# Two ways to transpose the inputs of tiles 8 to 15: on TensorE through PSUM, or on VectorE in 32x32 blocks put in place over DRAM

## The chip, the cores and the metric

The kernel runs on one core of a Trainium2 chip. The metric is the device time of one execution in microseconds; the median of a few executions is what counts. The engines are named as the profile names them: PE (TensorE) with its weight loads PEld, DVE (VectorE), ACT (ScalarE), POOL (GpSimd) and SP (SyncE, which here does nothing but issue DMAs; the profile writes SPq for its queue). Each engine takes its own instructions in order. Here that order is written out by hand for every engine.

## What is computed

Two layers with a residual sum each. The first mixes the 32 rows of a batch by a 32x32 matrix that its condition picks; the second is paged attention with new keys and values beside the cached ones.

```python
W = weights[condition]
x = x + einsum('bct,bcd->bdt', x, W)                # x: 64 batches x 32 rows x 512

q, k, v = x @ Wq.T, x @ Wk.T, x @ Wv.T              # 32 query heads, 8 key heads of 128
q, k = rope(rmsnorm(q)), rope(rmsnorm(k))
kc, vc = k_cache[block_table], v_cache[block_table] # 512 cached rows of a batch
probs = softmax(where(valid, q @ [kc, k].T * SCALE, -1e30))
x = x + (probs @ [vc, v]) @ Wo.T
```

All of it is float32.

## The kernel before

**Tiles, steps, slots.** The 2048 rows of x make 16 tiles of 128 rows (four batches of 32 rows: BT = 4, S = 32). The 8 key heads are taken in two halves of four. So there are 32 steps: steps 0 to 15 are tiles 0 to 15 with the first half of the heads, steps 16 to 31 the same tiles with the second half. The loop at L1549 gives each step 16 slots, one for each of its four batches and four units of scores. In a slot PE does one unit of scores against cached keys (`scores`, L1020), then what is planned for this slot (the dictionaries `plan`, `ahead` and `after_plan`, filled by `at`, L1342, and `later_of`), then the product with cached values of the slot before (`values`, L1081). Planned work is the preparation of later tiles and the output projection of earlier ones.

**The input of a tile.** Before the projections, a tile's rows have to be mixed with the condition matrix, added to themselves and transposed, so that the 512 inputs lie on the partitions: `x1t`, 128 partitions x 4 chunks x 128 rows. This is made once, in the first half, and kept in DRAM (`x1t_d`) for the second half. `input_of` (L1357) plans it: load the condition's blocks (`load_cond_weights`), load the rows (`x1_a`), mix (`x1_c`: one matmul of 128x512 on PE, an addition on DVE), transpose (`x1_b`, L411: four 128x128 transposes on PE into PSUM, one copy by ACT into SBUF). After `KEEP` = 2 slots the mixed rows go to `acc_d` (`keep_x1`, L428) and `x1t` goes to `x1t_d` (`keep_x1t`, L425), both issued by SP.

**Pairs.** From tile 4 on, tiles are projected in pairs by a seven-product scheme (`products`, L686). The two `x1t` of a pair are the four quarters A11, A12 (first tile) and A21, A22 (second tile) of one SBUF tile, `early`; there is only one such tile. `sums_x` (L665) makes S1 = A21 + A22 and S2 = S1 - A11 (L668, L669, slot 2 of step n), then S4 = A12 - S2 and S3 = A11 - A21 (L671, L672, slot 3). S3 is written over A21, so L672 has to wait until `keep_x1t` of the second tile has read it. The next DVE instruction in this slot is T2 (`t2`, L725), the difference of two weights. PE's product 6, S2 times T2 (`pb`, L697), stands in slot 5.

**Where the inputs stand.** A pair of tiles s0 and s0 + 1 is projected from step n = s0 - 2 on, and its inputs are made in step n - 1. For tiles 8 to 15 that is steps 5, 7, 9 and 11. There the mixing stood in slots 11 and 12 and the transposes in slots 13 and 14, while slots 9 to 13 also hold the last products of the output projection of two earlier tiles (`p67`, `p4_of`, L836), which wait for weight differences by DVE (L906, L907, L911).

**Cached keys.** SP loads a batch's cached keys in two halves of eight DMAs of 64 KB each (`load_k`, L312, DMAs at L321) into three buffers, the first half in the first and the second in the third slot of a batch, two batches ahead. Before each first half it loads the page numbers into its registers (L301). DVE copies the keys head by head (L1017, `kh`), four slots before PE needs them. The columns of queries come back from DRAM over SP as well (`spread`, L546, DMAs at L552).

**A block transpose that is there already.** The projected queries and keys are transposed without PE: `turn_rows` (L535) turns 32x32 blocks by DVE (L540, 128x512), POOL stores the result to `heads_d` with one DMA (L544), and `spread` loads it with the blocks in place. The buffer is `slab`, or in some slots `pn`, which is also where `new_scores` (L1040) puts its weights in slot 0 of each step.

POOL also gathers the cached values (L354, two in every second slot) and does part of the norm (L487, L488).

Of the kernel before, what the change touches and what calls it, by code (L numbers as in the profile page):

```python
# [12 lines left out]
F32 = mybir.dt.float32  # L13
# [7 lines left out]
P = 128  # L21
B, S, HID = 64, 32, 512
# [6 lines left out]
BT = P // S  # L29
NT = B // BT  # L30
# [3 lines left out]
KC = HID // P  # L34
# [26 lines left out]
def cond_resid_paged_attention_kernel(  # L61
# [23 lines left out]
    nc = tc.nc  # L85
# [3 lines left out]
    dram = ctx.enter_context(tc.tile_pool(name="dram", bufs=1, space=DRAM))  # L89
# [27 lines left out]
    part = const.tile([P, 1], F32, tag="part", name="part")  # L117
# [62 lines left out]
    def other_half(by):  # L180
# [2 lines left out]

    x1t_d = [
        dram.tile([P, KC * P], F32, tag=f"x1t_d{t}", name=f"x1t_d{t}") for t in range(NT)
    ]
    acc_d = [dram.tile([P, HID], F32, tag=f"acc_d{t}", name=f"acc_d{t}") for t in range(NT)]
    rot_d = {
# [14 lines left out]
    def steps_of(exact, pools):  # L203
        def pool(name, bufs, **kw):
            return pools.enter_context(
                tc.tile_pool(name=f"{name}_{int(exact)}", bufs=bufs, **kw)
            )
# [4 lines left out]
        work = pool("work", 2)  # L212
# [71 lines left out]
        def load_cond_weights(t, eng=nc.sync, kind=mybir.EngineType.SP):  # L284
            number = conditions(t, kind)
            for i in range(BT):
                blk = slice(i * S, (i + 1) * S)
                eng.dma_start(
                    bds[t % 2][blk, blk],
                    w_cond.rearrange("(n s) e -> n s e", s=S)[bass.ds(number[i], 1)].rearrange(  # L290
                        "o s e -> (o s) e"
                    ),
                )
# [89 lines left out]
        def x1_a(st):  # L383

            if st.pair is None:
                tag = "sums" if st.n and not exact else "acc"
                st.acc = work.tile([P, HID], F32, tag=tag, name=f"acc_{st.name}", bufs=2)
            else:
                i = st.n % 2
                if i == 0:  # L390
                    st.pair.read = work.tile(
                        [P, 2, HID], F32, tag="os", name=f"read_{st.name}", bufs=1
                    )
                st.acc = st.pair.read[:, i]
            src = acc_d[st.t] if st.hh else x[st.t * P : (st.t + 1) * P, :]
            nc.sync.dma_start(st.acc, src)
# [7 lines left out]
        def x1_c(st):  # L404
            if st.hh:
                return
            pm = ps_p.tile([P, 512], F32, tag="pp", name=f"pmix_{st.name}")
            nc.tensor.matmul(pm, bds[st.t % 2], st.acc, start=True, stop=True)
            nc.vector.tensor_tensor(st.acc, pm, st.acc, ALU.add)

        def x1_b(st):  # L411
            if st.hh:
                return
            pm = ps_p.tile([P, KC, P], F32, tag="pp", name=f"px1t_{st.name}")
            for c in range(KC):
                nc.tensor.transpose(pm[:, c, :], st.acc[:, c * P : (c + 1) * P], ident)
            if st.pair is None:
                st.x1t = work.tile(
                    [P, KC, P], F32, tag="x1t" if exact else "u3", name=f"x1t_{st.name}", bufs=1
                )  # L420
            nc.scalar.copy(st.x1t, pm)
            if st.n or exact:
                kept.append(lambda: keep_x1t(st, nc.sync))

        def keep_x1t(st, eng):  # L425
            eng.dma_start(x1t_d[st.t], st.x1t.rearrange("p c q -> p (c q)"))

        def keep_x1(st, eng=nc.sync):  # L428
            eng.dma_start(acc_d[st.t], st.acc)
# [103 lines left out]
        kept, in_slots = [], []  # L533
# [123 lines left out]
        def pair_x(pair):  # L657
            pair.x = early.rearrange("p (i c q) -> p i c q", i=7, c=2)
            for i, st in enumerate(pair.both):
                st.x1t = pair.x[:, 2 * i : 2 * i + 2].rearrange("p a c q -> p (a c) q")  # L660

        def load_x(st):
            nc.sync.dma_start(st.x1t.rearrange("p c q -> p (c q)"), x1t_d[st.t])
# [18 lines left out]
        def shift_w(hh, k):  # L682
            b11, _, b12, _ = halves(hh, k)
            nc.vector.tensor_tensor(b12, b12, b11, ALU.subtract)
# [135 lines left out]
        class Both:  # L820
# [123 lines left out]
            t = None  # L944
# [393 lines left out]
        for pair in pairs:  # L1338
            pair_x(pair)
        plan, ahead, after_plan = (defaultdict(list) for _ in range(3))  # L1340

        def at(n, slot, *work_of):  # L1342
            plan[n, slot].extend(work_of)
# [13 lines left out]
        def input_of(st, n, load, weights, mix, turned_at):  # L1357
            at(weights[0], weights[1], lambda: load_cond_weights(st.t))
            if load:
                at(load[0], load[1], lambda: x1_a(st))  # L1360
            at(n, mix, lambda: x1_c(st))
            at(n, turned_at, lambda: x1_b(st), lambda: kept.append(lambda: keep_x1(st)))

        def set_of(pair, k, n, slots):
            pieces = products(pair, k)
            for slot, names in slots.items():
                for name in names.split():
                    at(n, slot, pieces[name])
# [45 lines left out]
        for pair in pairs:  # L1414
            s0, s1 = pair.both
            n = s0.n - 2
            if n == 2:
                input_of(s0, 2, (1, 15), (1, 15), 4, 5)
                input_of(s1, 2, None, (2, 2), 6, 7)
                ahead[2, 1].append(lambda st=s1: x1_a(st))  # L1420
                at(2, 8, lambda: shift_w(0, 0))
                at(2, 9, lambda pair=pair: sums_x(pair))
                angles_of(2, 1, 9, 9)
                tables_of(pair, "q", 2, 8)
                tables_of(pair, "k", 3, 2)
                set_of(pair, 0, 2, {9: "t2", 10: "1", 11: "6 2 t3", 12: "5 t4", 13: "3 7", 14: "4"})
                at(3, 1, lambda: shift_w(0, 1))
                set_of(pair, 1, 3, {2: "t2", 3: "1 6 t3", 4: "2 5 t4", 5: "3", 6: "7", 7: "4"})
                at(3, 6, lambda: shift_w(0, 2))
                set_of(  # L1430
                    pair, 2, 3,
                    {8: "t2 1", 9: "2 t3", 10: "6 t4", 11: "7", 12: "4", 13: "5", 14: "3"},
                )
                spread_of(s0, 3, (12, 12, 13, 13))
            else:
                at(n, 2, lambda pair=pair: sums_x(pair, (0,)))
                at(n, 3, lambda pair=pair: sums_x(pair, (1,)))
                if pair.hh:
                    at(n - 1, 7, lambda st=s0: load_x(st))
                    at(n - 1, 10, lambda st=s1: load_x(st))  # L1440
                    tables_of(pair, "q", n - 1, 6)
                    tables_of(pair, "k", n, 7)
                else:
                    late = int(n == 4)
                    m = (n - 1, 7)
                    input_of(s0, n - 1, m, (n - 1, 6), 11 + 3 * late, 13 + 2 * late)
                    input_of(s1, n - 1, m, (n - 1, 7), 12 + 2 * late, 14 + late)
                    angles_of(s0.n // 2, n - 1, 4, 4 if late else 6)
                    if late:
                        tables_of(pair, "q", n, 1)  # L1450
                        tables_of(pair, "k", n, 4)
                    else:
                        tables_of(pair, "q", n - 1, 6)
                        tables_of(pair, "k", n, 11)
                if s0.n == NT:
                    at(n, 1, lambda: shift_w(1, 0))
                    at(n, 8, lambda: shift_w(1, 1))
                    at(n + 1, 3, lambda: shift_w(1, 2))
                set_of(
                    pair, 0, n,  # L1460
                    {3: "t2 1", 4: "2", 5: "6", 6: "5 t3", 7: "3 t4", 8: "7", 9: "4"},
                )
                set_of(
                    pair, 1, n,
                    {10: "t2", 11: "1", 12: "6 2 t3", 13: "5 t4", 14: "7 3", 15: "4"},
                )
                set_of(
                    pair, 2, n + 1,
                    {4: "t2 1", 5: "2 t3", 6: "6 t4", 7: "7", 8: "4", 11: "5", 13: "3"},
                )  # L1470
                spread_of(s0, n + 1, (10, 10, 11))
                ahead[n + 1, BT - 1].append(lambda st=s0: spread(st, BT - 1))
            spread_of(s1, n + 2, (3, 5, 8))
            ahead[n + 2, BT - 1].append(lambda st=s1: spread(st, BT - 1))
# [16 lines left out]
        valued, turned = (batch, GH - 1), [batch]  # L1491
# [57 lines left out]
        for st in steps:  # L1549
            for bt in range(0 if st.n else 1, BT):  # L1550
# [3 lines left out]
                for g in range(GH):  # L1554
# [39 lines left out]
                    if slot == (14 if st.n - 1 in twos else 10):  # L1594
# [4 lines left out]
                        turned = []  # L1599
# [16 lines left out]
                    if slot == 0 or slot == 13 and st.n - 1 not in twos or slot == 15:  # L1616
                        for ba in turned:
                            turn(ba)
                        turned = []
# [81 lines left out]
```

## Time and profile before

| | us |
|---|---|
| median of three executions | 2082.15 |
| the three | 2078.98, 2082.15, 2083.43 |
| the profiled execution | 2077.26 |
| span of the profiled execution, first to last instruction | 2075.5 |
| mean granted TensorE clock in it | 0.997 |
| one step (start of the new scores to the next), steps 5 to 12 | 62.4 to 65.1 |

The profiled execution ran 2077.26 us, 1.8 us more than its span, and 4.9 us less than the median of the three executions.

Busy time by step, for the four steps in which the inputs of tiles 8 to 15 are made and the four after them, from the view of windows:

| step | window, us | PE | PEld | DVE | ACT | POOL | share of DMA engines |
|---|---|---|---|---|---|---|---|
| 5 | 396 to 461 | 64.62 | 53.49 | 57.75 | 31.22 | 33.45 | 0.66 |
| 6 | 461 to 523 | 62.00 | 46.98 | 50.26 | 30.84 | 33.93 | 0.74 |
| 7 | 523 to 588 | 64.95 | 53.90 | 58.19 | 32.11 | 33.29 | 0.66 |
| 8 | 588 to 650 | 62.00 | 46.98 | 50.52 | 29.96 | 33.37 | 0.72 |
| 9 | 650 to 714 | 64.00 | 53.07 | 57.10 | 31.83 | 32.32 | 0.63 |
| 10 | 714 to 776 | 62.00 | 47.10 | 50.30 | 30.22 | 34.53 | 0.75 |
| 11 | 776 to 840 | 63.98 | 52.92 | 57.10 | 31.55 | 33.01 | 0.64 |
| 12 | 840 to 902 | 62.00 | 47.10 | 50.39 | 30.43 | 33.33 | 0.81 |

How to read the profile: a row of the timeline has its start and its length in microseconds, the engine and the line, what is written from what, the shape, how many instructions were merged, and in brackets the idle time before it with what ended it. A float32 matmul of the program runs as two matmul records, a transpose as one. Matmuls overlap in the pipeline, so that the length of one (273 ns for a transpose) is more than what it adds to PE's time; the chain of waits shows the latter.

### The profile page before, as it was taken

The page shows a single profiled execution, that of the slowest core. Times are in us where ns is not written, and L with a number is a line of the kernel's source. Part 1 is how long each engine was busy: PE and PEld are TensorE (multiplying, and loading weights), DVE is VectorE, ACT ScalarE, POOL GpSimd, SP SyncE. Part 2 cuts the span into 40 slices and gives each one's busy share as a digit, 9 for nine tenths or more (in the row PEclk, how much of TensorE's full clock was granted, in tenths as well). Part 3 has the DMA queues.
Part 4 walks back from the last instruction along what each step waited for, and adds up shares of the span by engine and source line. Part 5 has one row for each costly group of instructions (what it writes and reads, how often), then busy time and mean ns, then how long its engine had stood idle before and what let it go on. Part 6 is the DMA issues. An engine that isn't in the chain of part 4 may idle for free.

```text
span 2075.5 us, 45239 instructions
## 1 busy us (share of the span) xinstructions
PE 2042.3 (98%) x13428; PEld 1587.7 (76%) x13428; DVE 1630.7 (79%) x3532; ACT 958.4 (46%) x2707; POOL 991.2 (48%) x1122
## 2 busy tenths in 40 slices
PE   7999999999999999999999999999999999999998
PEld 4767667787887878878786677878878787787886
DVE  4555687988979789797997769889797987979744
ACT  4444354544545444544534445344454434545441
POOL 4354465545636465463544436355353544535331
PEclk9999999999999999999999999999999999999999
DMA  8767557667676676787767876676767667676672
GB/s 245 202 177 219 160 153 230 183 190 220 186 218 188 195 215 189 220 264 217 222 193 201 241 212 184 201 207 179 209 184 211 188 195 211 178 215 182 191 212 78
DMA packets 410255, 413.33 MB, mean 199 GB/s; under 512 B 58928, under 2 KB 325552, under 8 KB 410000
## 3 DMA queue, kind: packets, MB, share of 16 engines
q1 hardware_dynamic: 354096, 229.87, 39.1%
q0 software_dynamic: 55168, 180.27, 28.9%
q8 instruction: 109, 1.79, 0.4%
q14 instruction: 146, 1.20, 0.2%
q10 hardware_dynamic: 736, 0.21, 0.0%
HBM read 350.09 MB, written 60.03 MB: 198 GB/s over the span
## 4 chain that ended last, share of the span: by engine, by line
PE 80%; DVE 6%; DMA 6%; SPq 4%; issue 2%; POOL 1%; ACT 1%; DVEq 0%; ACTq 0%; POOLq 0%
PE ps_x L1026 18%; PE po_x L1089 18%; PE p_x L836 14%; PE pb_x L697 8%; PE pc_x L697 6%; PE pa_x L697 6%; PE pout_x L793 4%; SPq L321 3%; DMA k_t_x<-in_kt_dram 2%; PE pnv_x L1071 2%; PE pp_q_x L470 2%; PE psn_x L1047 1%; DMA q_ring_x<-heads_d 1%; PE pp_v_x L470 1%; DMA wq_x<-in_wq_dram 1%
## 5 line engine op out<-in xcount | busy, mean ns | idle before, releaser
L354 POOL DMA_INDIRECT raw_x<-in_vc_dram,v_row x512 | 548.3, 1071 | 639.8 <-ACT v_ring_x L366 518.4
L1037 ACT ACTIVATE pr_x<-ps_x 128x512 f32<-128x512 f32 x511 | 305.7, 598 | 779.1 <-PE ps_x L1026 774.1
L1089 PEld LDWEIGHTS po_x<-v_ring_x,pr_x 128*128 128x128 f32 x4088 | 522.9, 191 | 86.8 <-issue 66.2
L1026 PE MATMUL ps_x<-q_ring_x,kh_x 128*128 128x128 f32 x4088 | 546.4, 276 | 1.6 <-ACT q_ring_x L611 1.6
L1089 PE MATMUL po_x<-v_ring_x,pr_x 128*128 128x129 f32 x4088 | 543.5, 275 | 3.2 <-DVE nv_x L1100 2.8
L1026 PEld LDWEIGHTS ps_x<-q_ring_x,kh_x 128*128 128x128 f32 x4088 | 498.7, 192 | 13.8 <-issue 3.1
L366 ACT ACTIVATE v_ring_x<-raw_x,valid 128x512 f32<-128x512 f32 x512 | 342.7, 714 | 19.8 <-DMA raw_x<-in_vc_dram,v_row 19.2
L1017 DVE COPY kh_x<-k_t_x 128x512 f32<-128x512 f32 x506 | 219.8, 435 | 97.6 <-PE ps_x L1026 67.2
L544 POOL DMA_DIRECT2D heads_d<-rows_x x150 | 126.2, 842 | 280.8 <-DVE rows_x L540 215.9
L697 PE MATMUL pb_x<-t_x,early 128*128 128x512 f32 x504 | 238.2, 595 | 2.0 <-DVE u_x L713 1.1
L1100 DVE TENSOR_TENSOR nv_x<-po_x,nv_x 128x258 f32<-128x258 f32 x256 | 106.9, 417 | 100.7 <-PE po_x L1089 96.1
L836 PEld LDWEIGHTS p_x<-wo_x,ot_x 128*128 128x128 f32 x624 | 116.5, 190 | 62.3 <-issue 45.9
L488 POOL TENSOR_TENSOR rs_q_x<-ms_q_x,minus_half 128x4 f32<-128x4 f32 x128 | 158.8, 1241 | 10.7
L836 PE MATMUL p_x<-wo_x,ot_x 128*128 128x256 f32 x624 | 156.3, 380 | 0.1
L836 PE MATMUL p_x<-ts_x,ot_x 128*128 128x256 f32 x624 | 145.6, 380 | 0.7 <-DVE ts_x L911 0.7
L697 PEld LDWEIGHTS pb_x<-t_x,early 128*128 128x128 f32 x504 | 86.2, 191 | 64.8 <-issue 61.9
L836 PEld LDWEIGHTS p_x<-ts_x,ot_x 128*128 128x128 f32 x624 | 115.4, 190 | 25.3 <-issue 8.4
L1103 DVE TENSOR_TENSOR nv_x<-nv_x,rden 128x256 f32<-128x256 f32 x256 | 109.6, 428 | 8.7
L479 ACT ACTIVATE sq_q_x<-u_x 128x128 f32<-128x128 f32 x224 | 66.2, 298 | 94.0 <-DVE u_x L713 94.0
L697 PE MATMUL pc_x<-wq_x,early 128*128 128x512 f32 x224 | 105.4, 593 | 0.0
L697 PE MATMUL pa_x<-wq_x,early 128*128 128x512 f32 x224 | 105.4, 593 | 0.0
L514 DVE TENSOR_TENSOR rope_q_x<-rope_q_x,rs_q_x 128x512 f32<-128x512 f32 x120 | 82.3, 686 | 19.8 <-POOL rs_q_x L488 19.3
(203 smaller groups left out, 2612.0 us busy)
## 6 DMA issues: line engine op xcount, KB each, us to landing
k_t_x<-in_kt_dram SPq DMA_DIRECT2D x2048, 64.0 KB
heads_d<-rows_x POOLq DMA_DIRECT2D x150, 256.0 KB
q_ring_x<-heads_d SPq DMA_DIRECT2D x480, 80.0 KB
raw_x<-in_vc_dram,v_row POOLq DMA_INDIRECT x512
wo_x<-in_wo_dram SPq DMA_DIRECT2D x32, 256.0 KB
res_x<-acc_d SPq DMA_DIRECT2D x31, 256.0 KB
wq_x<-in_wq_dram SPq DMA_DIRECT2D x8, 512.0 KB
early<-x1t_d SPq DMA_DIRECT2D x16, 256.0 KB
```

What stands on the lines that cost most here:

```text
L354: nc.gpsimd.indirect_dma_start(out=raw.rearrange("p g d -> p (g d)"), out_offset=None, in_=vc, in_offset=bass.IndirectOffsetOnAxis(ap=v_ro ...
L366: nc.scalar.activation(v_ring[:, c, :, 0:D], raw, AF.Copy, scale=valid[:, b, c : c + 1])
L488: nc.gpsimd.tensor_tensor(rs, ms, minus_half, ALU.pow)
L544: nc.gpsimd.dma_start(heads_d[st.n][:, :, i, :].rearrange("k p c -> p k c"), part)
L697: nc.tensor.matmul(bank, pair.x[:, i, c, :], by[:, c * 512 : (c + 1) * 512], start=start and c == 0, stop=c == 1, skip_group_check=not start,)
L836: nc.tensor.matmul(to, left[:, i, :], right(i), start=start and i == 0, stop=i == QH // 2 - 1, skip_group_check=True,)
L1017: nc.vector.tensor_copy(to, src)
L1026: nc.tensor.matmul(ps[:, c, i, :], ba.k[j][:, i, c, :], queries(ba, g + i), start=True, stop=True,)
L1037: nc.scalar.activation(pr, ps, AF.Exp, scale=SCALE)
L1089: nc.tensor.matmul(ba.po[g][:, i, :], ba.pr[j][:, c, i, :], ba.v_t[:, 2 * half + c, g + i, :], start=(half == 0 and c == 0 and i == 0), st ...
L1100: nc.vector.tensor_tensor(t, ba.po[g], t, ALU.add)
L1103: nc.vector.tensor_tensor(t[:, :, 0:D], t[:, :, 0:D], rd.unsqueeze(2).to_broadcast([P, 2, D]), ALU.mult,)
```

## The change

For tiles 8 to 15 the four PE transposes and the ACT copy of `x1_b` are left out. In their place:

- `turn_x`: DVE turns the mixed rows in 32x32 blocks into a tile in the buffer `pn`, and POOL stores it to DRAM (`turned_d`) with four DMAs, one for each batch (each 32 partitions x 4 pieces of 512 bytes);
- `load_turned`: SP loads it into `x1t` with four DMAs, one for each chunk of inputs (each 128 partitions x 4 pieces of 128 bytes).

The mixing of the two tiles moves from slots 11 and 12 to 9 and 10, the turning from 13 and 14 to 10 and 12, and the loads stand in slots 12 and 14. `keep_x1t` is now asked for by `load_turned`: for the first tile it falls in slot 14, for the second in slot 0 of the next step, as before. `keep_x1` follows the turning by two slots, so it falls in slots 12 and 14. Tiles 0 to 7 are made as before.

```diff
+        def turn_x(st):
+
+            part = work.tile([P, 4, KC, S], F32, tag="pn", name=f"turned_{st.name}", bufs=1)
+            nc.vector.transpose(
+                part.rearrange("p k c s -> p c k s"),
+                st.acc.rearrange("p (c k d) -> p c k d", c=KC, k=4),
+            )
+            for b in range(BT):
+                nc.gpsimd.dma_start(
+                    turned_d[st.t].rearrange("(k d) b c s -> b d k (c s)", k=4)[b],
+                    part[b * S : (b + 1) * S].rearrange("d k c s -> d k (c s)"),
+                )
...
+        def load_turned(st):
+            for c in range(KC):
+                nc.sync.dma_start(
+                    st.x1t[:, c, :].rearrange("p (b s) -> p b s", b=BT), turned_d[st.t][:, :, c, :]
+                )
+            kept.append(lambda: keep_x1t(st, nc.sync))
...
-            at(n, turned_at, lambda: x1_b(st), lambda: kept.append(lambda: keep_x1(st)))
+            turned = x1_b if st.n < 8 else turn_x
+            at(n, turned_at, lambda: turned(st), lambda: kept.append(lambda: keep_x1(st)))
...
-                    input_of(s0, n - 1, m, (n - 1, 6), 11 + 3 * late, 13 + 2 * late)
-                    input_of(s1, n - 1, m, (n - 1, 7), 12 + 2 * late, 14 + late)
+                    mixes = ((14, 15), (14, 15)) if late else ((9, 10), (10, 12))
+                    input_of(s0, n - 1, m, (n - 1, 6), *mixes[0])
+                    input_of(s1, n - 1, m, (n - 1, 7), *mixes[1])
+                    if not late:
+                        at(n - 1, 12, lambda st=s0: load_turned(st))
+                        at(n - 1, 14, lambda st=s1: load_turned(st))
```

The rest of the diff declares `turned_d`, one DRAM tile of 128 x 4 x 4 x 32 floats for each tile of rows. The flag `late` is set for the pair of tiles 6 and 7 alone.

More of the change, by code (lines that the diff above doesn't have):

```diff
@@ L185, in cond_resid_paged_attention_kernel @@
         dram.tile([P, KC * P], F32, tag=f"x1t_d{t}", name=f"x1t_d{t}") for t in range(NT)
+    ]
+    turned_d = [
+        dram.tile([P, BT, KC, S], F32, tag=f"turned_d{t}", name=f"turned_d{t}") for t in range(NT)
     ]
```

## The prediction

> **What bounds the kernel now.** I read the busy times first, then the chain of waits.
>
> ```profile
> PE 2042.3 (98%) x13428; PEld 1587.7 (76%) x13428; DVE 1630.7 (79%) x3532; ACT 958.4 (46%) x2707; POOL 991.2 (48%) x1122
> PE 80%; DVE 6%; DMA 6%; SPq 4%; issue 2%; POOL 1%; ACT 1%; DVEq 0%; ACTq 0%; POOLq 0%
> ```
>
> PE is the bound, so work taken off PE should shorten the run, unless PE then waits. From 546 to 898 us the chain never leaves PE. The part of it around the first two removed transposes (start, what it adds to the chain) shows their price:
>
> ```profile
> 454.22 0.44 PE px1t_x L416 x4
> 454.65 0.87 PE p_x L836 x4
> ...
> 457.31 0.44 PE px1t_x L416 x4
> ```
>
> A tile's four transposes last 273 ns each but add only 0.44 us together. Next I read SP's timeline at the same place, because the change gives SP new work:
>
> ```profile
> 452.48 9.45 SPq L321 DMA_DIRECT2D k_t_x<-in_kt_dram  x16
> 462.04 0.84 SPq L967 DMA_DIRECT2D acc_d<-res_x  x2
> 462.97 0.43 SPq L426 DMA_DIRECT2D x1t_d<-early  x1
> 463.46 0.77 SPq L429 DMA_DIRECT2D acc_d<-read_x  x1
> 467.31 4.69 SPq L321 DMA_DIRECT2D k_t_x<-in_kt_dram  x8
> 472.11 0.37 SPq L426 DMA_DIRECT2D x1t_d<-early  x1
> ```
>
> SP issues without a rest here. The keys issued at 452.48 go into a buffer that DVE emptied with its copy at 442.02: SP is some 10 us behind what it could do. The hole from 464.23 to 467.31 is a load of page numbers (L301), not a wait. The last row is the second tile's `keep_x1t`, and DVE and PE hang on it. DVE's timeline, then PE's:
>
> ```profile
> 475.75 0.42 DVE L672 TENSOR_TENSOR early<-early 128x256 f32<-128x256 f32 x1 [3.74 <-DMA x1t_d<-early]
> 476.10 1.22 DVE L725 TENSOR_TENSOR t_x<-wq_x 128x1024 f32<-128x1024 f32 x1
> ```
>
> ```profile
> 478.16 1.88 PE L697 MATMUL pb_x<-t_x,early 128*128 128x512 f32 x4
> ```
>
> DVE idled 3.74 us until that store had read A21; T2 was ready at 477.32 and PE's product 6 began at 478.16. So SP may be 0.84 us later before PE stops. The same rows for the other three pairs: T2 ready 599.73, product 604.40 (4.67 us room; L672 at 598.17 did not wait); 730.24 and 730.65 (0.41; L672 had waited 4.18); 853.38 and 856.86 (3.48; waited 1.11).
>
> **The change, part by part.**
>
> Removed: 32 transposes, 8 tiles x 0.44 = 3.5 us off PE's path, 0.87 a pair. Eight ACT copies (L421, 0.586 us each, 4.7 in all) go too; ACT is 46% busy and PE does not wait for it there, so they bring nothing.
>
> Moved: the mixing (two records, 0.86 us of PE a tile) goes two slots ahead at the same cost. In slot 10, p67's second weight difference ended at 436.16 on DVE and PE wanted it at 436.63; the move puts 0.69 of addition (L409) ahead of it on DVE and 0.86 on PE, so the room grows by 0.17. PE now wants the loaded rows some 8 us earlier. Their issue ended at 427.68, 554.19, 681.97 and 806.67, the mixing will stand at about 431.9, 558.5, 684.7 and 811.1. SP's stores landed 2.2 to 3.5 us after issue (475.75, 728.68 and 851.82 against issues that ended at 472.48, 725.17 and 849.59), so only the third is in doubt, by 0.8 us at most; I take 0.
>
> Added on DVE: eight block transposes at 0.71 us (L540, same shape), 5.7 us. They stand in slots 10 and 12, and behind them DVE idles for PE four times by 1.0 to 1.1 us (444.65, 449.89, 451.64, 454.25), which holds 1.42 a pair. Without that cover the cost would be 1.42 a pair. The second one has to wait until the four stores of the first have read `pn`.
>
> Added on POOL: 32 stores. A 128-row store of 1 KB rows took 0.605 us (L462 median), one of 512 pieces 0.834 (L544): 2.4 to 3.3 us a tile, nearer 2.4. The first four, at about 440, push a row store (440.37) and two gathers (441.90, 443.25) back by 2.4; ACT used those at 453.09, so nothing waits. The second four fall in POOL's hole of 9.85 us before 454.07.
>
> Added on SP, the part that decides: eight loads a pair, all ahead of the second tile's `keep_x1t`, and the second `keep_x1` (0.42 plus 0.05 of gap), which stood behind it, moves ahead too. No row shows a load of 128 x 4 pieces of 128 bytes. The nearest in form, 128 x 2 or 4 pieces of 2 KB (L264), took 468 ns in the middle and 378 to 1112 at the ends:
>
> ```profile
> L264 SPq DMA_DIRECT2D wq_x<-in_wq_dram x11: 378/468/1112, 1.7 to 913.1; - x11
> L301 SPq TENSOR_LOAD <-pages_sb x128: 968/1002/3102, 11.0 to 2021.2; - x128
> ```
>
> With 0.05 between issues that is 8 x 0.52 + 0.47 = 4.6 us by which SP reaches `keep_x1t` later. Upper bound 8 x 1.16 + 0.47 = 9.8, if the small pieces drain so badly that SP is held each time. Lower bound: 8 x 0.43 + 0.47 = 3.9, less what the long page load could give back (2.8 to 3.1 us behind four stores in a row in three pairs, 1.0 usually), so 2.0. I take 4.6: the middle row of the nearest form, on a queue that issues back to back.
>
> [...]
>
> Who waits then: SP's new loads wait for POOL's stores (landed by about 446, SP there at 457), so they do not hold the keys behind them. The keys of slot 14 are issued 2.6 us later and reach DVE about in time (5.1 us before). The second tile's load lands near 470, DVE's S1 wanted it at 467; that wait ends before the one at L672. There DVE stands 4.6 later; behind it are T2, a key copy and the additions that free PSUM, and PE waits for T2. A pair loses 4.6 less its room, and cannot gain more than 0.87. First pair 4.6 - 0.84 = +3.8. Second: room 4.67 plus the unseen lead of the store (issue end 594.11 + 2.2 to 3.5 = 596.3 to 597.6, against 598.17), -0.8. Third 4.6 - 0.41 = +4.2. Fourth 4.6 - 3.48 = +1.1. Behind these points DVE waits for PE (484.45, 488.81), so the loss stays.
>
> **Sum.** +8.3 us on the profiled 2077.3 gives 2085.6, 0.40% more. On the median of the three, 2082.15, that is 2090.5, which I give as the time.
>
> **Rivals.**
>
> *SP has room after all (not slower).* The page load shrinks, or the new issues fit into time in which SP is held by the DMA engines anyway (single issues there took 1.75 and 1.25). If SP comes less than 0.4 us later, all four pairs keep 0.87: -3.5 us, 2078.7. It decides below 1.6 us of lateness, where the sum crosses zero (0.8 - 0.9 + 1.2 - 0.9). For it: the 2 us excess of the page load. Against: eight issues cost at least 3.4 by any row of SP. Between 1.6 and 3.3 us the loss is 0 to 4.
>
> *The small pieces hold SP.* About 0.95 us an issue, 8 us late: 7.2 + 2.6 + 7.6 + 4.5 = +22 us, 2104. For it: the issue behind two loads of 256 pieces of 2 KB took 1.3 us at 881.7. Against: there 1 MB had to drain, here 64 KB.
>
> *DVE's second transpose waits for `pn`.* The first tile's stores end their issue near 442.4; with 3.5 to land that is 446, and DVE asks at 449. Only from a landing past 452 would PE's p4 (454.5) stop, with some 2 us a pair, +8 beside the rest: 2098.
>
> *The change does something else than it says.* The old way stays for tiles below 8, the new loads are left out for 6 and 7; the 32 transposes are gone from PE's order. Not likely.
>
> **How the numbers follow.** Forecast, SP 3.3 to 6 us late (+4 to +14): 0.50. Less than 3.3: 0.25, of it most within 4 us of no change. Held SP: 0.20. `pn`: 0.05. About 0.2%, 4.2 us, is what a measurement of this kernel tells from no change (the three runs spread by 0.2%). Even the full gain of 3.5 is below that, so faster 0.05, same 0.20, slower 0.75. The range leaves out a tenth at each end: 2080 (a full gain with some loss) to 2104 (SP held).
>
> **What would show it.** Right: L672 waits for `x1t_d<-early` in pairs one, three and four by more than before, with PE idle before `pb` by about 4.7, 0.1, 5.1 and 2.0 us (lateness less room, plus 0.87). SP's eight loads at about 0.47 each. Transposes and mixing elsewhere unchanged, `px1t` 32 fewer. Wrong: no PE idle before `pb`, L672 where it was; or PE idle at `pmix`, `p_x` or `po` in slots 9 to 13, which would be DVE or the rows; or issues of 1 us.

## The result and the profile after

The changed kernel takes 2099.74 us (median of six runs, 2096.23 to 2102.94) where the kernel before takes 2080.46 on the same chip: ratio 1.0096, 95% interval 1.0081 to 1.011. It is slower by some 20 us by this ratio. The forecast was slower by 8.3 us, at 2090.5, with a range of 2080 to 2104. The profiled run of the changed kernel took 2102.84 us (span 2101.0), 25.6 us more than the profiled run before; the traces are compared with that difference in mind.

Where the difference lies is seen from the steps, each from one start of the new scores (`psn`) to the next:

| step | 5 | 6 | 7 | 8 | 9 | 10 | 11 | 12 | sum |
|---|---|---|---|---|---|---|---|---|---|
| before, us | 65.1 | 62.4 | 63.8 | 62.4 | 63.8 | 62.4 | 63.8 | 62.4 | 506.1 |
| changed, us | 63.9 | 72.3 | 62.9 | 69.8 | 62.9 | 70.2 | 63.3 | 66.4 | 531.7 |

All of it falls in these eight steps; outside them the differences cancel. (The changed kernel is 1.5 us ahead when step 5 begins, gains 3.1 us in the later steps, and loses 4.5 at the end, where its granted clock is 0.5 for 6.83 us from 2030.0 us and that of the kernel before is 1.00 from 2000 to 2071.) The odd ones, which lost their PE transposes, are shorter by 3.5 us together, just as forecast. The even ones, where the pairs are multiplied, are longer by 29.1. The page of the changed kernel, busy time, then the chain of waits by engine:

```profile
PE 2045.8 (97%) x13396; PEld 1586.9 (76%) x13396; DVE 1633.9 (78%) x3540; ACT 953.1 (45%) x2699; POOL 1011.9 (48%) x1154
PE 73%; DVE 8%; SPq 7%; DMA 6%; issue 3%; POOL 1%; ACT 1%; DVEq 0%; ACTq 0%; POOLq 0%
```

PE has 32 instructions fewer and yet 3.5 us more of busy time, and PE's share of the chain has fallen from 80% to 73%, of which DVE and SP's queue have taken 5. SP's timeline in the first pair shows why (line numbers are now those of the changed kernel; L680 is the new load, L445 and L442 are `keep_x1` and `keep_x1t`, L990 stores the residual rows of two earlier tiles):

```profile
455.75 0.43 SPq L445 DMA_DIRECT2D acc_d<-read_x  x1
456.37 2.67 SPq L680 DMA_DIRECT2D early<-turned_d  x4
459.28 4.46 SPq L324 DMA_DIRECT2D k_t_x<-in_kt_dram  x8
463.78 0.43 SPq L445 DMA_DIRECT2D acc_d<-read_x  x1
464.25 0.43 SPq L442 DMA_DIRECT2D x1t_d<-early  x1
464.87 3.43 SPq L680 DMA_DIRECT2D early<-turned_d  x4
468.40 3.07 SPq L990 DMA_DIRECT2D acc_d<-res_x  x2
474.10 3.96 SPq L324 DMA_DIRECT2D k_t_x<-in_kt_dram  x8
478.11 0.43 SPq L442 DMA_DIRECT2D x1t_d<-early  x1
```

Four loads take 2.67 and 3.43 us, 0.67 and 0.86 each, not 0.52. And the two stores behind them, 0.84 us before, now take 3.07; one of the two is 2.59 long by itself. (In the third pair they took 2.29 before and 2.02 now.) From the keys behind the sixteen `q_ring` loads (450.65 here) to the end of the second `keep_x1t` SP needs 27.9 us, against 20.0 before. In the four pairs it is 7.9, 8.8, 7.6 and 7.4 us later. DVE, at the same place:

```profile
472.31 0.42 DVE L691 TENSOR_TENSOR early<-early 128x256 f32<-128x256 f32 x1 [5.72 <-DMA early<-turned_d]
...
481.77 0.42 DVE L695 TENSOR_TENSOR early<-early 128x256 f32<-128x256 f32 x1 [6.84 <-DMA x1t_d<-early]
482.11 1.22 DVE L748 TENSOR_TENSOR t_x<-wq_x 128x1024 f32<-128x1024 f32 x1
```

DVE now waits twice: at S1 for the load, and at S3 for the store. T2 is ready at 483.33, and PE's product 6 begins at 483.39, after an idle of 7.73 us. PE's timeline, then DVE's and PE's waits in the four pairs (total, times, longest):

```profile
483.39 3.78 PE L720 MATMUL pb_x<-t_x,early 128*128 128x512 f32 x4 [7.73 <-DVE t_x L748]
```
```profile
DVE early L695 <- DMA x1t_d<-early: 22.2, 4, 6.8
DVE early L691 <- DMA early<-turned_d: 19.1, 4, 5.7
```
```profile
PE pb_x L720 <- DVE t_x L748: 19.7, 4, 7.7
```

In the four pairs PE idles 7.73, 4.72, 5.25 and 2.02 us there, 19.7 in all. The four matmul records of product 6 take 3.78 us, where the kernel before took 1.88: the prediction had no term for what follows the idles. The windows around the ends of the four idles (after the busy times: granted clock, share of the DMA engines, GB/s):

```profile
479.00:488.00 9.00, 4.61 (x9) 2.45 (x10) 5.98 (x14) 0.00 (x0) 0.61 (x1) 0.62 0.83 243
612.00:621.00 9.00, 5.42 (x12) 3.10 (x13) 6.75 (x15) 0.77 (x2) 2.03 (x2) 0.62 0.82 243
745.00:754.00 9.00, 5.19 (x10) 2.89 (x11) 6.52 (x15) 0.47 (x1) 2.04 (x2) 0.62 0.81 243
878.00:884.00 6.00, 4.84 (x13) 2.83 (x14) 5.90 (x13) 1.05 (x2) 2.29 (x2) 0.72 0.74 230
```

The granted clock falls to 0.5, for 6.83 us from 480.4, 613.5 and 746.6, and for 3.41 us from 879.8. In the kernel before it is 1.00 from 400 to 900 us. An estimate: if the parts of those spells that lie behind the idles cost PE half their length, they cost 1.9 + 2.4 + 2.3 + 1.7 = 8.3 us (product 6 of the first pair alone lost 1.9). With it the difference is made up: 19.7 of idle + 8.3 of slow clock - 3.5 of transposes = 24.5 of the 25.6 us.

### The profile page after: what moved, and what is told of

Read it like the earlier page. It is cut to its first block, busy times and chain, and to the rows that moved or that the text cites. A ratio compares the mean times of both kernels' runs of the same rounds, so it can differ in the third digit from the quotient of the medians.

```text
span 2101.0 us, 45306 instructions
## 1 busy us (share of the span) xinstructions
PE 2045.8 (97%) x13396; PEld 1586.9 (76%) x13396; DVE 1633.9 (78%) x3540; ACT 953.1 (45%) x2699; POOL 1011.9 (48%) x1154
## 4 chain that ended last, share of the span: by engine, by line
PE 73%; DVE 8%; SPq 7%; DMA 6%; issue 3%; POOL 1%; ACT 1%; DVEq 0%; ACTq 0%; POOLq 0%
PE ps_x L1049 17%; PE po_x L1112 17%; PE p_x L859 12%; PE pb_x L720 8%; PE pc_x L720 6%; SPq L324 5%; PE pa_x L720 4%; PE pout_x L816 4%; DMA k_t_x<-in_kt_dram 4%; PE pp_q_x L486 2%; PE pnv_x L1094 1%; DVE kh_x L1040 1%; PE psn_x L1070 1%; SPq L568 1%; PE pp_v_x L486 1%
## 5 line engine op out<-in xcount | busy, mean ns | idle before, releaser
L720 PE MATMUL pb_x<-t_x,early 128*128 128x512 f32 x504 | 245.3, 610 | 23.3 <-DVE t_x L748 22.0
```

Of the source, the lines that this page charges most:

```text
L720: nc.tensor.matmul(bank, pair.x[:, i, c, :], by[:, c * 512 : (c + 1) * 512], start=start and c == 0, stop=c == 1, skip_group_check=not start,)
```

## Experiments

Theory A is that SP, held by the loads of small pieces, comes late to the second `keep_x1t`, and S3, T2 and PE follow. Each run was timed against the kernel before on the same chip. "Eight steps" is the sum for steps 5 to 12 in the profiled run (before 506.1, changed 531.7).

### Is it the pieces, or the number of loads?

```diff
-                    st.x1t[:, c, :].rearrange("p (b s) -> p b s", b=BT), turned_d[st.t][:, :, c, :]
+                    st.x1t[:, c, :], turned_d[st.t][:, c].rearrange("p c s -> p (c s)")
```

> Same eight loads a pair in the same places, each 128 rows of 512 contiguous bytes in place of 128 x 4 pieces of 128 bytes. Left out: the exchange of blocks, so tiles 8 to 15 get their rows in another order; the work after it is the same. If the small pieces make the price (theory A1): an issue takes about 0.45 us and not 0.67 to 0.86, the res stores behind them 0.9 and not 1.5 to 3.1 us, SyncE comes some 4 us earlier to the second keep_x1t than in the changed kernel, PE idle before pb 3.5, 0.5, 1.5 and 0 us, time 12 to 16 us below the changed kernel (near the forecast's own sum, 2084 to 2088). If it is the number of issues (A2): 0.67 us or more each, idle and time as in the changed kernel within 4 us.

Measured: ratio 1.0032 (1.0015 to 1.005), 6.7 us above the kernel before and some 13 below the changed one; eight steps 517.4. The second run has one load a tile:

```diff
-            for c in range(KC):
-                nc.sync.dma_start(
-                    st.x1t[:, c, :].rearrange("p (b s) -> p b s", b=BT), turned_d[st.t][:, :, c, :]
-                )
+            nc.sync.dma_start(
+                st.x1t.rearrange("p c q -> p (c q)"),
+                turned_d[st.t].rearrange("p b c s -> p (b c s)"),
+            )
```

> One load a tile, 128 rows of 2 KB, in place of four of 128 x 4 x 128 bytes, keep_x1t where it was. Left out: the exchange of blocks, as above. Theory A: SyncE's burden before the second keep_x1t is 2 x 0.43 + 0.47 = 1.3 us, below every room but the first and third (0.84, 0.41 us), PE idle before pb about 1.4, 0, 1.7, 0 us, time 2077 to 2082, about 20 us below the changed kernel. Theory B: DVE still waits for the store and the load, because stores and loads through memory take 3 us each to land, whatever their number: PE idle of 2 us a pair or more stays, time at most 12 us below the changed kernel.

Measured: ratio 0.9997 (0.9983 to 1.0011); eight steps 508.8. The groups of the load, in order the changed kernel, pieces of 512 bytes, one load (min/median/max of an issue in ns):

```profile
L680 SPq DMA_DIRECT2D early<-turned_d x32: 524/630/1308, 456.4 to 865.7; - x32
```
```profile
L680 SPq DMA_DIRECT2D early<-turned_d x32: 322/384/952, 457.6 to 853.0; - x32
```
```profile
L679 SPq DMA_DIRECT2D early<-turned_d x8: 320/332/1051, 458.7 to 843.2; - x8
```

The same number of loads and of bytes: 32 issues took 22.5 us in the changed kernel and 14.0 in 512-byte pieces, and the two stores behind them went back from 9.1 us (four pairs) to 3.8. SP's second `keep_x1t` was 7.9 us later in the mean with small pieces, 5.1 with larger ones, 3.2 with one load; PE idled 19.7, 8.8 and 4.2 us for T2; the time is 20, 7 and 0 us above the kernel before. A1 holds for the most part: with larger (and so fewer) pieces some 13 of the 20 us go, though SP comes 2.8 us earlier and not 4, and PE idles 2.80, 2.01, 2.24 and 1.76 us, not 3.5, 0.5, 1.5 and 0. The rest goes with the number of loads; with one load a tile the 4.2 us of idle stand against the 3.5 saved. How long the two stores are held varies: behind the same small loads on SP they took 3.9 (e1), 5.1 (e11) and 7.0 us (e9) in the four pairs, against 4.45 in the kernel before.

### The burden alone, and the move alone

The kernel before, with eight loads of the small form and no other part of the change:

```diff
+        def burden(pair):
+            to = pair.x[:, S1 : S2 + 1].rearrange("p a c q -> p (a c) q")
+            rows = x1t_d[0].rearrange("p (b c s) -> p b c s", b=BT, c=KC)
+            for c in range(KC):
+                nc.sync.dma_start(to[:, c, :].rearrange("p (b s) -> p b s", b=BT), rows[:, :, c, :])
...
+                        at(n - 1, 12, lambda pair=pair: burden(pair))
+                        at(n - 1, 14, lambda pair=pair: burden(pair))
```

> The kernel before, complete with TensorE's transposes and ScalarE's copies, with nothing but SyncE's burden of the changed kernel: eight loads a pair of 128 x 4 pieces of 128 bytes in slots 12 and 14, from rows long written, into the place that S1 and S2 will overwrite. Theory A: SyncE's issues take 0.6 to 0.9 us each, the second keep_x1t comes 6 to 8 us later than in the kernel before, S3 waits, PE idles before pb by some 5 to 7, 2 to 4, 5 to 6 and 2 us, with half-speed spells: 16 to 24 us above the kernel before, so the loss of the change is wholly SyncE's. Rival H (the turn over memory as such, its stores on GpSimd, DVE's second transpose or the rows' late arrival makes the loss): less than 8 us above the kernel before.

Measured: ratio 1.0074 (1.0054 to 1.0095), 15.4 us; eight steps 522.2. The issues took 0.62 us in the median, SP was 6.0, 7.6, 5.2 and 6.7 us later, and the waits of the four pairs, DVE's and then PE's (us in total, times, longest), were:

```profile
DVE early L680 <- DMA x1t_d<-early: 28.3, 4, 8.1
```
```profile
PE pb_x L705 <- DVE t_x L733: 10.2, 4, 3.6
```

The loss comes without a turn over memory, just below the range given. PE's idle is 9.5 us shorter than the change's: SP is 1.5 us a pair less late, and PE, still doing its transposes, comes 0.9 us a pair later to the wait. And only two of the four idles (2.30, 2.40, 3.61, 1.93 us), the last two, were followed by a granted clock of 0.5. Against this stand the 3.5 us of the transposes, which this run still pays. Now the move alone:

```diff
-                    input_of(s0, n - 1, m, (n - 1, 6), 11 + 3 * late, 13 + 2 * late)
-                    input_of(s1, n - 1, m, (n - 1, 7), 12 + 2 * late, 14 + late)
+                    mixes = ((14, 15), (14, 15)) if late else ((9, 10), (10, 12))
+                    input_of(s0, n - 1, m, (n - 1, 6), *mixes[0])
+                    input_of(s1, n - 1, m, (n - 1, 7), *mixes[1])
```

> The kernel before, with mixing and TensorE's transposes of tiles 8 to 15 moved to the slots where the changed kernel has them (mixing 9 and 10, transposes 10 and 12); no turn over memory. The prediction's step that the move costs nothing: time within 0.2% of the kernel before (2077 to 2085), and S3's waits of 3.7 and 4.2 us gone, as the store is issued some 5 us earlier. Rival: the move itself costs, since PE asks for the mixing's rows and DVE's addition earlier: PE idle at pmix or p_x in slots 9 to 12, 4 us or more above the kernel before.

Measured: ratio 1.0003 (0.9992 to 1.0014). The second `keep_x1t` is out at 458.57 instead of 472.48, no wait for it is left among DVE's, and nothing is gained: that wait was covered before. The step priced at nothing costs nothing.

### Is the store the last link?

```diff
-            kept.append(lambda: keep_x1t(st, nc.sync))
+            rows = st.pair.both[0]
+            kept.append(
+                lambda: nc.sync.dma_start(x1t_d[st.t], rows.x1t.rearrange("p c q -> p (c q)"))
+            )
```

> The changed kernel, whose second store keep_x1t of a pair reads the first tile's rows (A11, A12) in place of its own (A21, A22); left out, so, are the second tile's own rows in the second half. SyncE issues exactly what it did, at the same places, and the loaded rows come as late as they did; only S3 over A21 need not wait for the store. Theory A (the store is the last link): S3's waits of 6.8, 5.1, 5.4 and 4.9 us gone, PE idle before pb about 0.9, 0, 0 and 0 us, no half-speed spells, time 2077 to 2082, some 20 us below the changed kernel. Theory B (the loads come too late by themselves): PE idle before pb 2 us a pair or more, time above 2088.

Measured: ratio 1.0055 (1.004 to 1.007), 11.4 us; eight steps 520.1. PE's waits for T2 went to 0.67, 0, 0 and 0, as theory A had them, but the time did not follow: it is above 2088, which was theory B's number, without theory B's idle. DVE waited for the loads at S1 (L694 here) as before, and T2 was in time all the same. DVE's largest waits and PE's (total, times, longest):

```profile
DVE early L694 <- DMA early<-turned_d: 19.2, 4, 5.9
DVE kh_x L1043 <- DMA k_t_x<-in_kt_dram: 13.2, 5, 3.9
```
```profile
PE pb_x L723 <- DVE u_x L739: 6.9, 3, 3.3
PE pc_x L723 <- DVE u_x L739: 2.5, 2, 1.5
```

For T2 the store was the last link, but another wait stood close behind it: with S3 free, DVE goes on to its key copy (L1043) and waits there for keys that the same late SP has issued, then comes late with the additions that free PSUM (L739). In the first pair T2 was ready at 476.08, and the key copy behind it began only at 479.67. A good half of the loss (11.4 of some 20 us) stays. The prediction let the keys arrive "about in time"; they do not.

### Another engine's queue for the store, the loads, or the other stores

Three runs take issues from SP to ScalarE. First `keep_x1t` of the turned tiles:

```diff
-            kept.append(lambda: keep_x1t(st, nc.sync))
+            kept.append(lambda: keep_x1t(st, nc.scalar))
```

> Only the queue of one store is changed: the eight keep_x1t of the turned tiles are issued by ScalarE, not by SyncE. Theory A (SyncE reaches the second tile's keep_x1t late, DVE's S3 waits for it, T2 and product 6 follow, and the PE clock falls after the idle): S3's waits of 6.84, 5.05, 5.41 and 4.90 us all but vanish, and as they are as long as or longer than PE's 7.73, 4.72, 5.25 and 2.02 us of idle before pb, these fall to about 0.9, 0, 0 and 0; no half-speed spell after them; time about 20 us below the changed kernel, so 2077 to 2082. Theory B (the loaded rows themselves come too late, DVE's wait of 3.4 to 5.7 us at S1 is what counts): S1 waits as before, PE idles before pb by 2 us or more a pair, time at most 8 us below the changed kernel.

Measured: 1.0155 (1.013 to 1.018), slower than the change. S3 waits for nothing any more and PE no longer stops at `pb`, as theory A had it, but its time is missed by 30 us. ScalarE stands in its order before the store until the load has landed, and the exponentials stand behind it. ACT's timeline:

```profile
468.27 0.33 ACTq L442 DMA_DIRECT2D x1t_d<-early  x1
468.70 0.60 ACT L1060 ACTIVATE pr_x<-ps_x 128x512 f32<-128x512 f32 x1 [5.81 <-DMA early<-turned_d]
```

PE idles at `po` for 21.4 us in the four pairs in place of 19.7 at `pb`. Then the loads as well:

```diff
             for c in range(KC):
-                nc.sync.dma_start(
+                nc.scalar.dma_start(
```

> The eight loads a pair and the two keep_x1t are issued by ScalarE; SyncE is left with less than in the kernel before. Theory A: SyncE early, PE never idles before pb, the removed transposes pay at last: 2 to 4 us below the kernel before, about 2076 to 2079. Rival C: 128 x 4 small pieces hold the issuing engine 0.67 to 0.86 us each wherever they are issued, so ScalarE stands 2.7 to 3.4 us a tile, its exponentials come late and PE waits for pr or v_ring: 1 to 3 us a tile, 8 to 24 us above the first theory's time.

Measured: 1.0138 (1.0115 to 1.016). An issue takes ScalarE 0.64 us in the median, as it took SP; but PE's idle is for DVE (15.5 us at `po`), DVE's is for keys (39.6 us), and SP, with less to do, is later: in the first pair the last of the sixteen `q_ring` loads is issued at 456.6, in the changed kernel at 448.8. The time, 2110.93, lies above both theories' numbers. Last, with the loads back on SP, the two `keep_x1` and the two `res` stores on ScalarE:

```diff
-            at(n, turned_at, lambda: turned(st), lambda: kept.append(lambda: keep_x1(st)))
+            eng = nc.sync if st.n < 8 else nc.scalar
+            at(n, turned_at, lambda: turned(st), lambda: kept.append(lambda: keep_x1(st, eng)))
...
-                        store(twos[st.n - 1].s0)
-                        store(twos[st.n - 1].s1)
+                        eng = nc.scalar if st.n in (7, 9, 11, 13) else nc.sync
+                        store(twos[st.n - 1].s0, eng)
+                        store(twos[st.n - 1].s1, eng)
```

> The changed kernel; SyncE is relieved of other work in front of the second keep_x1t: the two keep_x1 and the two res stores of each of the four pairs (some 0.9 and 1.5 to 3.1 us) are issued by ScalarE; the loads of small pieces stay. Theory A (how late SyncE is decides, whichever issue makes it late): SyncE comes 3 to 4 us earlier than in the changed kernel, PE idle before pb about 3, 1, 3 and 0 us in place of 7.7, 4.7, 5.3 and 2.0, time 8 to 16 us below the changed kernel, 2084 to 2091. Rival G (the loads' own landing or the DMA engines under small pieces decide): PE idles about as in the changed kernel, time within 5 us of it. ScalarE may wait for res or for the rows; then PE idles at po.

Measured: 1.0152 (1.0132 to 1.0172), a miss of 24 us or more for theory A's number. The waits of SP in the four pairs (total, times, longest):

```profile
SPq L568 <- DMA acc_d<-read_x: 21.1, 4, 6.9
SPq L324 <- DMA acc_d<-read_x: 13.3, 4, 3.9
```

By the profile's account SP stands 34.4 us for ScalarE's stores of x1 to land, in front of its loads of query columns (L568) and keys (L324), which share no data with those stores. In the run before (e4), the same two lines waited 32.4 us for ScalarE's loads and 12.4 for its stores. What ties them is open. So these runs say nothing on whether a lighter SP would have helped; they say that in both the issues moved to ScalarE's queue came back as a wait of SP.

### Other ways to place the pieces

Sixteen stores on GpSimd, straight into the layout that is read, one load, no `keep_x1t`:

```diff
-            for b in range(BT):
-                nc.gpsimd.dma_start(
-                    turned_d[st.t].rearrange("(k d) b c s -> b d k (c s)", k=4)[b],
-                    part[b * S : (b + 1) * S].rearrange("d k c s -> d k (c s)"),
-                )
+            to = x1t_d[st.t].rearrange("(k d) (c b s) -> b k d c s", k=4, c=KC, b=BT)
+            for b in range(BT):
+                for k in range(4):
+                    nc.gpsimd.dma_start(to[b, k], part[b * S : (b + 1) * S, k])
```

> The 128-byte pieces move from SyncE's loads to GpSimd's stores: 16 stores a tile (32 rows of 4 pieces of 128 bytes) straight into the place that the second half reads anyway, one load a tile of 128 rows of 2 KB on SyncE, no keep_x1t for tiles 8 to 15. Theory A: SyncE issues two loads in place of two keep_x1t, S3 waits for no store; PE never idles before pb; the 32 removed transposes show, 3 to 6 us below the kernel before: 2075 to 2079. Rival D: 16 issues of 0.4 to 0.6 us on GpSimd (6 to 10 us a tile) push gathers back, ScalarE fills v_ring late and PE idles at po by 2 to 5 us a tile: 2095 to 2120. Rival E: 128-byte pieces are dear on any queue because they slow the DMA engines for the keys, as when ScalarE issued the loads: DVE waits for k_t, time about the changed kernel's.

Measured: 1.0104 (1.0086 to 1.0121). Rival D: GpSimd, then ScalarE behind its gathers, each from its timeline:

```profile
450.15 8.71 POOL L438 DMA_DIRECT2D x1t_d<-turned_x  x15
```
```profile
462.97 0.72 ACT L369 ACTIVATE v_ring_x<-raw_x,valid 128x512 f32<-128x512 f32 x1 [5.55 <-DMA raw_x<-in_vc_dram,v_row]
```

PE never waits for T2 there, and idles 3.3 to 3.8 us a pair (not 2 to 5 a tile) at `po` instead, each time with a granted clock of 0.5. The other way gives the store and the load long pieces by a layout with the chunk innermost:

```diff
-                    pp, st.x1t[:, c, :], w[:, c, :], start=(c == 0), stop=(c == KC - 1)
+                    pp, st.x1t[:, :, c], w[:, c, :], start=(c == 0), stop=(c == KC - 1)
...
-                        pair.x[:, i, c, :],
+                        pair.x[i][:, :, c],
...
-            part = work.tile([P, 4, KC, S], F32, tag="pn", name=f"turned_{st.name}", bufs=1)
+            part = work.tile([P, 4, S, KC], F32, tag="pn", name=f"turned_{st.name}", bufs=1)
```

> The transposed rows are laid out with the four 128-wide chunks innermost ([p, token, chunk]), so that a store of GpSimd and a load of SyncE both have pieces of 512 bytes or more without any further shuffle: the four stores a tile go straight to where the second half reads, one load a tile of 2 KB rows, no keep_x1t for tiles 8 to 15. TensorE reads its weights for the products with a step of 16 bytes (8 for the sums). Theory A: SyncE has nothing more to do than before, S3 waits for no store, the removed transposes show: 3 to 6 us below the kernel before, 2075 to 2079. Rival F: the stepped weight loads (1,500 of them, 190 ns each at present, hidden behind matmuls) or the stepped sums, copies and transposes on DVE and ACT get slower: if a weight load doubles to 0.4 us, PE waits some 0.1 to 0.2 us at each, 150 to 300 us above.

Measured: 1.008 (1.0062 to 1.0098). The eight steps take 507.7 us and PE waits for nothing in the pairs: SP's part of the loss is gone. Rival F took the gain, at a tenth of the size feared and in most steps of the run: PE is busy 2064.5 us against 2045.8, and its matmuls of `pa` last 617 to 622 ns in the mean, not 593. (In this profile 6.4 us more than in the changed kernel's fall in step 18 alone, where two short idles were followed by a granted clock of 0.5; why PE stopped there is open.) Groups of weight loads (step of 16 bytes, then of 8), and for comparison the changed kernel's:

```profile
L717 PEld LDWEIGHTS pa_x<-wq_x,early x224: 307/309/338, 236.3 to 1903.8; 128*128 128x128 f32 x112
L717 PEld LDWEIGHTS pc_x<-wq_x,early x224: 194/197/198, 245.1 to 1912.7; 128*128 128x128 f32 x112
```
```profile
L720 PEld LDWEIGHTS pa_x<-wq_x,early x56: 189/190/192, 467.6 to 873.5; 128*128 128x128 f32 x56
```

### What the slow clock costs

Unread matmuls ahead of product 6 keep PE busy while it waits for T2:

```diff
                 t["b"] = bank("pb")
+                fill = {8: 8, 10: 4, 12: 5, 14: 1} if k == 0 else {}
+                for _ in range(fill.get(s0.n, 0)):
+                    nc.tensor.matmul(t["b"], pair.x[:, A11, 0, :], w(B11)[:, 0:512], start=True, stop=True)
                 product(t["b"], S2, t[2], True)
```

The first try had the numbers 14, 8, 9 and 2, keyed to tiles 6, 8, 10 and 12:

> The changed kernel, with matmuls that nobody reads (14, 8, 9 and 2 of 128x512, 0.47 us each) ahead of product 6 of the first weight set in the four pairs, so that PE is busy for all but about 1 us of the 7.7, 4.7, 5.3 and 2.0 us for which it waited there; the wait for T2 itself stays. If the half-speed spells after the idles are caused by the idles and cost time (theory A's second part): no granted clock of 0.5 after 480, 613, 746 and 880 us, the first four products pb at 1.88 us again, time 7 to 12 us below the changed kernel, 2088 to 2093. If the slow clock costs nothing that the wait does not cover already: time as the changed kernel's within 2 us.

Measured: 1.0141 (1.0124 to 1.0157). It filled the wrong pairs; 12.18 us of unread matmuls stood where PE waited for nothing. It does show one thing: in the first two of the four pairs the waits were filled whole by the matmuls meant for others, and the granted clock stayed at 1.00 (windows from 480 to 505 and 612 to 632 us). The second try:

> The run before filled the wrong pairs (the first 14 matmuls stood in the pair of tiles 6 and 7, which waits for nothing) and an unread 128x512 matmul took 0.86 us there, two records each, not 0.47. Now 8, 4, 5 and 1 of them stand in the pairs of tiles 8/9, 10/11, 12/13 and 14/15: 6.9, 3.4, 4.3 and 0.9 us of the 7.7, 4.7, 5.3 and 2.0 us of wait. If the idles cause the half-speed spells and these cost time beside the wait: no clock of 0.5 between 400 and 900 us, time 7 to 12 us below the changed kernel, 2087 to 2093. If the spells cost nothing more: within 2 us of the changed kernel.

Measured: 1.0083 (1.0066 to 1.01), which overlaps the changed kernel's interval. In its profile the waits of the first two pairs were filled whole, there was no idle and the granted clock was 1.00 (478 to 490 and 607 to 613 us), and steps 6 and 8 took 69.3 and 65.9 us in place of 72.3 and 69.8: 3.0 and 3.9 less. PE in the first pair:

```profile
475.60 7.03 PE L771 MATMUL pb_x<-wq_x,early 128*128 128x512 f32 x16
482.47 1.88 PE L720 MATMUL pb_x<-t_x,early 128*128 128x512 f32 x4
```

In the other two pairs the wait was longer in this run than the fill, 3.35 and 2.51 us of idle were left, the granted clock fell (mean 0.70 from 741 to 747 us, 0.72 from 874 to 880), and the steps took 73.2 and 67.7 (70.2 and 66.4). So in this run the fall came with the idle, and where PE was kept busy there was none. What that saves can't be read from these steps: counted from the step's start, SP ended the store 1.9 and 3.4 us earlier than in the changed kernel's profile in the first two pairs, so that T2 was ready (480.17, 609.88) before the fill was through, and 1.1 and 1.8 us later in the other two. That it would give 7 to 12 us over the whole run is not shown.

No version beat the kernel before. The most that the idea can give here is the 3.5 us of the transposes, 0.17%, and each way to place the blocks cost more than that.

## Why the prediction was right, and where it was too small

- **Direction and place: right.** PE stops at product 6 in the four pairs, for the reason named: SP late, `keep_x1t`, S3, T2, product 6. Only the second pair, for which 0.1 us of idle was forecast, stops by 4.72. The burden alone gives 15.4 us (e11), one load a tile no loss (e3).
- **Removed transposes: right**, -3.5 us in the odd steps. **Move: right**, nothing (e7). **DVE's transposes** took 0.70 us (0.71 forecast) and **POOL's stores** 0.58 each (0.605 taken); no wait for `pn` stands among DVE's.
- **SP's lateness: mis-sized.** The term "8 x 0.52 + 0.47 = 4.6" measured 7.9 in the mean. An issue of 512 small pieces took 0.70 in the mean, 0.75 with the gap behind it, not 0.47 and 0.52 (the row L264 has 256 or 512 pieces of 2 KB a load; its four loads by SP with 512, as many pieces as here, took 0.38 to 0.73 at the start of the run, so it is not the count of pieces alone that was missed; e2 changed count and size together, and no run parts them), and the two stores behind them 1.15 us a pair more, a cost that the sum didn't have (and that varies from run to run). This is the lateness of the rival in which small pieces hold SP (8 us), reached by 0.75 an issue and held stores in place of 0.95 an issue. The time lies in the range because the range reached up to this rival, which was given a chance of 0.20. That the rival's +22 us is near the 20 measured is partly luck: its four terms stand for 25.4 us of idle and no slow clock, the trace has 19.7 of idle, and 8.3 of slow clock by the estimate above. With loads of 128 pieces of 512 bytes (e2), whose issue took 0.44 in the mean, near the term's 0.47, SP was 5.1 late and the loss 6.7 us, against 4.6 and 8.3.
- **Rooms: right, but SP's lateness is not S3's.** Lateness less room plus 0.87 gives 7.9, 5.0, 8.0 and 4.8 us of idle for the lateness measured; the trace has 7.73, 4.72, 5.25 and 2.02. Counted from the start of the step, S3 began 8.7, 9.5, 5.8 and 5.6 us later than before, and that less the rooms is 7.8, 4.8, 5.4 and 2.1, which fits. In the third pair S3 could start 1.74 us after the store's issue ended, not 3.51 as before; in the fourth SP began the stretch 1.8 us earlier, as counted from the step's start.
- **The clock: left out.** The sum counted an idle of PE at its length. Here, by the estimate above, the idles cost 8.3 us beyond it: the granted clock fell to 0.5 during the first three (4.72 to 7.73 us long), for 6.83 us each, and 0.6 us after the fourth (2.02 us long), for 3.41 us.
- **The keys: wrong**, as e9 shows; it didn't decide, since S3 held DVE longer.

In numbers: forecast 11.9 us of idle less 3.5; measured 19.7 less 3.5, and by estimate 8.3 of slow clock.

## What to carry to other kernels

Before work goes from a full engine to a queue, price that queue by issues whose pieces have the same number and size (a load of 64 KB held SP 0.63 us in pieces of 128 bytes and 0.38 in pieces of 512), and count what stands behind them too. Then list everybody who waits for that queue: when the first wait was taken away, in e9, the next stood close behind (13.2 us of DVE for keys). And an idle of some microseconds on PE cost its length here and, with 21 of 22 longer than 2.7 us, a granted clock of 0.5 during or after it.

## What the runs showed of the hardware

- **Idle and clock.** In the fourteen profiles, between 400 and 1990 us, PE had 22 idles longer than 2.7 us, and the granted clock fell to 0.5 during or after 21 of them (the one without a fall was 3.88 long, in e10); with 8 of 14 idles of 1.9 to 2.7 us; with none of seven of 1.4 to 1.9. Shorter ones were followed by a fall only twice, two close together each time (1.15 and 0.65 us, 1.12 and 0.65). The shortest idle that had a fall by itself was 1.93 us long (e11).
- **Pieces and issue.** The load of a tile's 256 KB held its queue 0.33 us as one DMA of 2 KB pieces, 0.38 for each of four in 512-byte pieces, 0.63 for each of four in 128-byte pieces (medians), and on ScalarE's queue much the same, 0.64. Four loads of 1 MB in 512 pieces of 2 KB, as many pieces as one of those four, took 0.38 to 0.73 in the kernel before (L264).
- **Stepped weights.** A weight load that reads every fourth float took 309 ns, every second 197 (both e8), every one 190 (the changed kernel); DVE's block transpose that writes every fourth float took 1.10 us (e8) and not 0.70.
- **Two queues.** By the profile's account SP waited for ScalarE's DMAs without a dependence of data, 34.4 us in four pairs (e10); the cause is open.
